# Layer 3 of a four-layer graph network: phases over neighbouring source blocks, turned pairs grouped by target, node operations on GpSimd

## The chip, the cores and the metric

The kernel is one launch on one core of a Trainium2 chip. The time is the device time of the launch in microseconds; for the kernel before it is 658.86 us, the median of 3 runs (657.34 to 660.25). Each engine of the core (TensorE for matrix products, VectorE, ScalarE and GpSimd for elementwise work, SyncE for transfers) runs its own instructions in the order in which the program issues them, and waits for the others through semaphores. The profile calls them PE (PEld for its weight loads), DVE, ACT, POOL and SP.

## The reference

The input is 3327 nodes of 64 features and a dense 3327 x 3327 matrix `adj`, mostly zero. Four layers follow one another: a gated graph network of two rounds, a hyperbolic one, one with rank weights, and a hyperbolic one with attention, which is the one changed. Each is added to `x`:

```python
h = jnp.maximum(_layernorm(x, axis=-1), 0.0)
x = x + _L3_gnn_ref(h, adj, L3_gnn_att_W, L3_gnn_att_b)

def _L3_gnn_ref(x, adj, att_W, att_b):
    x_tan = _logmap0(x, C)
    left = x_tan @ att_W[:D] + att_b
    right = x_tan @ att_W[D:]
    adj_att = jax.nn.sigmoid(left + right.T) * adj
    x_local = _logmap(x[:, None, :], x[None, :, :], C)
    support_t = jnp.einsum('ij,ijd->id', adj_att, x_local)
    return _proj(_expmap(x, support_t, C), C)
```

`_logmap(p1, p2)` of two nodes is a combination of both, with a factor that depends on their norms and distance. So every pair (i, j) needs a distance and an attention; but the distance is the same for (i, j) and (j, i).

## The kernel before

The nodes are padded to 26 blocks of 128. A column block `c` (0 to 12) is two of them, b = 0 and 1. Group `gs_` holds column blocks 0 to 5, group `gf` 6 to 12. Layers 0 to 2 stream `adj` from memory through the products; layer 3 reads `adj3`, a copy that the host lays out in the order of use.

Layer 3 works through 91 pairs of column blocks in 13 **phases** of 7 pairs (`Phase`, L131 on): four within `gf`, six between the groups (source one block of `gs_`, all seven of `gf` as targets), three within `gs_`. A phase has two halves b. A half takes these steps, each a function marked `step3`:

- `distances`: TensorE, in chunks of 4 and 3 pairs, into a pair of PSUM banks; `gelus` (ScalarE) brings them out through a Gelu, `square` (ScalarE) squares what is left: a fit of the factor of the logarithm. The result tile is s0 to s3.
- `tanh_d` (L1355), `attention_d` (L1392), `factors_d` (L1410): the attention of the direct pairs by a tanh on ScalarE, times `adj` and then times the factor on VectorE; `gather_d` and `singles` are the products that sum over sources (L1438, with the features `xd` and with `p2c`).
- the **turned** pairs, the same distance for the other direction: `turned` (L1422) transposes the squares 64 by 64 on TensorE into the other pair of banks; `tanh_t` (L1379) makes the attention, one instruction for each pair; `attention_t`, `factors_t` (L1429, reading PSUM) and `gather_t` follow, four pairs at a time (a chunk u). A pair of a block with itself has no turned one.

Before that the nodes need their own values. `nodes3` is a generator that runs once for each group and is advanced by the letters `n` (gf) and `s` (gs_): layer norm, norms, the transposed features `xs` and their swapped copy `xw` (four transfers issued by GpSimd), packed rows for the distances (`par`, `ab`, `pack`, then transposes to `rows_i` and `rows_j`), and `leftb`. For `gs_` it begins where layer 2 ends, while the phases within `gf` run. `b` is the bound that picks the fast ending, `f` the ending of `gf`; `finish` is that of `gs_`.

The order of all steps is written out by hand in `ORDER3` and is the order of each engine's queue. In it `distances.0.1.0` is phase 0, half 1, chunk 0; `factors_t.1.0.1` is phase 1, half 0, chunk 1. PSUM has two pairs of banks (`pair(0)` for distances, `pair(1)` for transposes) and four single banks; two of these, 2 and 3, take the first two distance chunks, of phase 0 half 0, before the sums of `gf` need them.

## Time and profile before

| | |
|---|---|
| median of 3 runs | 658.86 us |
| profiled execution, its time and span | 658.55, 656.7 us |
| TensorE busy, share of the span | 611.3 us, 93% |
| VectorE | 454.3 us, 69% |
| ScalarE | 386.2 us, 59% |
| GpSimd | 9.3 us, 1% |
| mean granted TensorE clock | 0.983 |
| layer 3, first distances to the end | 410 to 656.7 us |

A row of the profile names line, engine and operation, written tile <- read tiles, shape and count, then busy microseconds and mean nanoseconds of one. A product of two float32 operands is two TensorE instructions. Numbers in brackets behind a row of the timeline are the engine's idle time before it and what ended it. TensorE's ends are modelled, so the starts are the safer reading. Other layers are not touched by the change, except that the hand-written order also covers the end of layer 2.

### The profile page before, as it was taken

The numbers are of one execution on the slowest core, as the hardware profiler recorded it, in microseconds if no ns is written. First come the engines' busy times: TensorE is split into PE (matmuls) and PEld (weight loads), VectorE is DVE, ScalarE is ACT, GpSimd is POOL, SyncE is SP. The second block draws the span as 40 slices with busy tenths as digits, with TensorE's granted clock in tenths as the row PEclk, the third lists the DMA queues.
The fourth block names the chain that finished last, engine by engine and source line by source line (L and its number), as shares of the span: only waits on it lengthen the run. The fifth ranks groups of instructions, "written<-read, shape, count | busy, mean of one in ns | idle before, by whom it ended". The sixth has DMA issues, their size and how long they took to land.

```text
span 656.7 us, 14066 instructions
## 1 busy us (share of the span) xinstructions
PE 611.3 (93%) x6004; PEld 339.1 (52%) x6004; DVE 454.3 (69%) x721; ACT 386.2 (59%) x562; POOL 9.3 (1%) x19
## 2 busy tenths in 40 slices
PE   1987999999999999889999999799999999999993
PEld 1442344344333434346667677366666666676781
DVE  3240777345488740777656865789999999999966
ACT  3110400130253501368888889889999999999914
POOL 0000000000000000010000100010000000000000
PEclk9999999999999999999999999989999999999995
DMA  8999999359996999998879897426667665666501
GB/s 337 417 365 418 372 387 343 155 201 403 418 415 276 355 412 417 418 397 316 308 246 330 279 318 255 137 82 193 210 226 249 232 252 170 226 199 194 188 2 57
DMA packets 32534, 183.46 MB, mean 279 GB/s; under 512 B 3696, under 2 KB 4752, under 8 KB 32464
## 3 DMA queue, kind: packets, MB, share of 16 engines
q1 hardware_dynamic: 32112, 181.63, 74.1%
q0 software_dynamic: 352, 0.85, 0.5%
q8 instruction: 49, 0.80, 0.5%
q14 instruction: 21, 0.17, 0.1%
HBM read 180.76 MB, written 0.85 MB: 277 GB/s over the span
## 4 chain that ended last, share of the span: by engine, by line
PE 78%; ACT 7%; DMA 6%; DVE 6%; issue 2%; SPq 0%; ACTq 0%; DVEq 0%
PE bank L730 27%; PE bank L1438 17%; PE pair L1321 7%; PE pair L1763 7%; PE bank L1785 6%; DMA adj<-in_adj 5%; PE pair L1422 4%; PE pair L831 2%; ACT w L1775 2%; PE pair L635 1%; ACT tr L1379 1%; PE bank L1535 1%; DMA xn<-in_x 1%; ACT d L1355 1%; ACT dir L1355 1%
## 5 line engine op out<-in xcount | busy, mean ns | idle before, releaser
L730 PE MATMUL bank<-adj,m_a 128*64 128x384 f32 (+1 forms) x832 | 155.0, 519 | 9.3 <-DMA adj<-in_adj 6.9
L730 PEld LDWEIGHTS bank<-adj,m_a 128*64 128x64 f32 x832 | 57.1, 138 | 96.9 <-issue 72.3
L1775 ACT ACTIVATE w<-pair,ebias 128x896 uint16<-128x896 f32 (+1 forms) x100 | 91.2, 954 | 15.2 <-PE pair L1763 14.3
L730 PE MATMUL bank<-adj,m_b 128*64 128x384 f32 (+1 forms) x416 | 76.7, 515 | 1.4 <-ACT hm L819 1.4
L458 DVE SCALAR_TENSOR_TENSOR edges<-adj,edges 128x1792 bf16<-128x1792 f32 (+1 forms) x24 | 45.0, 1890 | 30.5 <-DMA adj<-in_adj 30.4
L1732 DVE TENSOR_SCALAR mask<-adj 128x1792 bf16<-128x1792 f32 (+1 forms) x52 | 52.0, 1027 | 17.2 <-PE pair L1763 17.2
L819 ACT ACTIVATE hm<-bank 64x384 f32<-64x384 f32 (+1 forms) x8 | 4.1, 512 | 94.5 <-DVE mh L818 94.3
L1785 PE MATMUL bank<-w,m_b 128*64 128x384 bf16 (+1 forms) x416 | 56.0, 340 | 0.0
L730 PEld LDWEIGHTS bank<-adj,m_b 128*64 128x64 f32 x416 | 29.0, 137 | 45.6 <-issue 42.4
L1321 PE MATMUL pair<-xs,xw 64*128 64x512 f32 (+3 forms) x116 | 50.3, 519 | 1.6 <-ACT sq L1337 1.1
L1321 PE MATMUL pair<-xs 64*128 64x512 f32 (+3 forms) x116 | 50.3, 519 | 1.3 <-ACT sq L1337 1.1
L1392 DVE SCALAR_TENSOR_TENSOR d<-d,adj 128x1792 f32<-128x1792 f32 x19 | 38.3, 2016 | 0.0
L1785 PE MATMUL bank<-w,h_t 128*64 128x384 bf16 x208 | 37.9, 339 | 0.0
L1763 PE MATMUL pair<-mask,tri_b 128*64 128x384 bf16 (+1 forms) x208 | 37.3, 339 | 0.0
L1355 ACT ACTIVATE d<-leftb,righth 128x1792 f32<-128x1792 f32 (+6 forms) x27 | 35.2, 1337 | 0.0
L1763 PE MATMUL pair<-mask,rest_a 128*64 128x384 bf16 x192 | 33.4, 341 | 1.8 <-ACT w L1775 1.6
L1379 ACT ACTIVATE tr<-leftb,righth 128x256 f32<-128x256 f32 x82 | 34.9, 499 | 0.3 <-PE bank L1438 0.3
L1438 PE MATMUL bank<-d,xd 128*64 128x384 f32 (+3 forms) x188 | 32.2, 472 | 0.0
L1785 PEld LDWEIGHTS <-m_b 128*64 128x64 bf16 x416 | 25.9, 110 | 12.3 <-issue 1.4
L1379 ACT ACTIVATE t<-leftb,righth 128x256 f32<-128x256 f32 x74 | 31.3, 499 | 0.2 <-PE bank L1438 0.2
L1438 PE MATMUL bank<-d,p2c 128*32 128x256 f32 (+1 forms) x304 | 29.6, 345 | 0.0
L1763 PE MATMUL pair<-mask,tri_a 128*64 128x384 bf16 x208 | 27.1, 341 | 1.7 <-ACT w L1775 1.6
(336 smaller groups left out, 1100.5 us busy)
## 6 DMA issues: line engine op xcount, KB each, us to landing
adj<-in_adj SPq DMA_DIRECT2D x108, 896.0 KB, 6.2
adj<-in_adj SPq DMA_DIRECT2D x92, 768.0 KB, 8.3
adj<-in_adj SPq DMA_DIRECT2D x12, 640.0 KB, 4.1
xn<-in_x SPq DMA_DIRECT2D x3, 192.0 KB, 5.2
out<-s SPq DMA_DIRECT2D x3, 192.0 KB, 2.4
xw<-xs POOLq DMA_DIRECT2D x4, 128.0 KB, 4.8
w_l<-in_w_l SPq DMA_DIRECT2D x1, 460.0 KB, 10.0
xn<-in_x SPq DMA_DIRECT2D x1, 256.0 KB, 6.8
```

Of the source, the lines that this page charges most:

```text
L458: V.scalar_tensor_tensor(e, a, 0.0, e, op0=OP.not_equal, op1=OP.add)
L730: T.matmul(acc[q][h * D : (h + 1) * D, : hi - lo], lhsT=m[:, k, :], rhs=a[:, h * g.w + lo : h * g.w + hi], start=first, stop=last,)
L1321: T.matmul(p[k][:, o : o + n], lhsT=l, rhs=r, start=not rows, stop=rows)
L1355: S.activation(columns(dirs[m, b], ph.n)[:, :, first * P : first * P + n], left_of(ph.g)[:, :, o : o + n], AF.Tanh, bias=righth[:, 2 * c + ...
L1379: S.activation(a[:, 8 * u * P : (8 * u + 2 * n) * P].rearrange("p (r x c) -> p x r c", r=2, c=D)[:, 2 * i : 2 * i + 2], left_of(ph.s)[:, : ...
L1392: V.scalar_tensor_tensor(a[:, :w], a[:, :w], 1.0, stream.tile(stream.now), op0=OP.add, op1=OP.mult)
L1422: T.transpose(p[:, r * 512 + o : r * 512 + o + D], a[rs], ident[rs, rs])
L1438: T.matmul(out, lhsT=lhsT, rhs=rhs, start=False, stop=True, skip_group_check=True)
L1732: V.tensor_scalar(masks[n][:, :w], a, 0.0, None, op0=OP.not_equal)
L1763: T.matmul(cnt[h][s * D : (s + 1) * D, P + lo : P + hi], lhsT=l, rhs=r, start=first and j == 0, stop=j == len(terms) - 1 or first and s == ...
L1775: S.activation(w, e, AF.Relu, bias=ebias)
L1785: T.matmul(acc2[i][q][h * D : (h + 1) * D, : hi - lo], lhsT=p[:, 2 * c + a, :], rhs=ws[n][:, h * g.w + lo : h * g.w + hi].bitcast(BF16), s ...
```

## The change

`Phase` takes several (source, targets) runs. Between the groups a phase now has two neighbouring sources, with four and three targets, in place of one source with seven; within the groups the 91 pairs are likewise cut anew. Turned pairs of one target block whose sources are neighbours form a group: one tanh, and products over both, where there was one for each. Chunks hold whole groups, up to four pairs. The first distance chunks lie in other banks: (phase 0, half 0, chunk 0) and (0, 1, 1) in the single banks, (0, 0, 1) in `pair(1)`. Phase 0's square is done on VectorE as a * (a + 2 HG), and the constant HG^2 is added with the next factor. In `nodes3` of `gs_`, `E` is GpSimd: the small operations on SBUF go there; copies from PSUM and the relu go to ScalarE. `singles` mixes direct and turned products by the columns done so far. The host's layout of `adj3` follows, and `ORDER3` is written anew.

```diff
@@ -132,28 +132,54 @@
 
 
 
-    def __init__(self, cs, targets):
-        self.runs = []
-        self.cols, self.turned = [], []
-        for c in cs:
-
-            ts = [o for o in targets if c not in targets or o >= c]
+    def __init__(self, *sources):
+        self.runs, self.cols = [], []
+        by_j = {}
+        for c, ts in sources:
+            ts = list(ts)
             self.runs.append((c, ts, len(self.cols)))
             for o in ts:
                 if o != c:
-                    self.turned.append((len(self.cols), c, o))
+                    by_j.setdefault(o, []).append((c, len(self.cols)))
                 self.cols.append((c, o))
-        self.g = next(g for g in GROUPS if targets[0] in g.cs)
-        self.s = next(g for g in GROUPS if cs[0] in g.cs)
-        self.n, self.nt = len(self.cols), len(self.turned)
-
-
-COLS = [list(g.cs) for g in GROUPS]
-PHASES = [Phase(cs, COLS[1]) for cs in ((9, 10), (8, 11), (7, 12), (6,))]
+
+        groups = []
+        for j, entries in by_j.items():
+            for c, i in sorted(entries):
+                if groups and groups[-1][0] == j and groups[-1][1] + groups[-1][2] == c:
+                    groups[-1][2] += 1
+                    groups[-1][3].append(i)
+                else:
+                    groups.append([j, c, 1, [i]])
+        groups.sort(key=lambda g: -g[2])
+        self.turned, x = [[]], 0
+        for j, c, n, i in groups:
+            if sum(g[2] for g in self.turned[-1]) + n > 4:
+                self.turned.append([])
+            self.turned[-1].append((j, c, n, i, x))
+            x += 2 * n
+        self.g = next(g for g in GROUPS if self.runs[0][1][0] in g.cs)
+        self.s = next(g for g in GROUPS if self.runs[0][0] in g.cs)
+        self.n, self.nt = len(self.cols), x // 2
+
+
+r_ = range
+PHASES = [
+    Phase((6, r_(6, 10)), (7, r_(7, 10))),
+    Phase((9, r_(9, 11)), (11, r_(11, 13)), (8, r_(8, 11))),
+    Phase((6, r_(10, 13)), (12, r_(12, 13)), (7, r_(10, 13))),
+    Phase((8, r_(11, 13)), (9, r_(11, 13)), (10, r_(10, 13))),
+]
 BETWEEN = len(PHASES)
-PHASES += [Phase((c,), COLS[1]) for c in COLS[0]]
+for _c in range(0, 6, 2):
+    PHASES.append(Phase((_c, r_(6, 10)), (_c + 1, r_(6, 9))))
+    PHASES.append(Phase((_c + 1, r_(9, 13)), (_c, r_(10, 13))))
 WITHIN = len(PHASES)
-PHASES += [Phase(cs, COLS[0]) for cs in ((0, 5), (1, 4), (2, 3))]
+PHASES += [
+    Phase((0, r_(0, 4)), (1, r_(1, 4))),
+    Phase((0, r_(4, 6)), (1, r_(4, 6)), (4, r_(4, 6)), (5, r_(5, 6))),
+    Phase((2, r_(2, 6)), (3, r_(3, 6))),
+]
 
 
...
+SINGLE3 = ((0, 0, 0), (0, 1, 1))
+BY_V3 = (0,)
...
-    weigh.51.0 weigh.49.1 weigh.50.1 weigh.51.1 wk distances.0.1.0 distances.0.1.1
-    attention_t.0.0 attention_d.0.0 tanh_t.0.1.1 attention_t.0.1 square.0.0 evict s clear.0
-    clear.2 gelus.0.1.0 clear.1 tanh_t.1.0.0 factors_d.0.0 distances.1.0.0 s s s gelus.0.1.1
-    square.0.1 turned.0.0.0 gelus.1.0.0 s distances.1.0.1 factors_t.0.0.0 turned.0.0.1 s s
...
+    count.51.0 count.51.1.1 weigh.49.1 distances.0.0.0 attention_t.0.0 gelus.0.0.0
+    distances.0.0.1 weigh.50.0 weigh.51.0 gelus.0.0.1 attention_d.0.0 square.0.0 weigh.50.1
+    weigh.51.1 wk evict distances.0.1.0 s s s tanh_t.1.0.0 gelus.0.1.0 tanh_d.0.1
+    distances.1.0.0 gelus.1.0.0 distances.0.1.1 s clear.2 distances.1.0.1 gelus.0.1.1 s
+    clear.1 factors_d.0.0 clear.0 square.0.1 gelus.1.0.1 gather_d.0.0 s s turned.0.0.0
+    factors_t.0.0.0 distances.1.1.0 gather_t.0.0.0 turned.0.0.1 attention_t.0.1
+    factors_t.0.0.1 gather_t.0.0.1 singles.0.0 s s tanh_d.1.0 turned.0.1.0 gelus.1.1.0
+    factors_t.0.1.0 distances.1.1.1 s turned.0.1.1 attention_d.0.1 factors_d.0.1 square.1.0
+    factors_t.0.1.1 gelus.1.1.1 distances.2.0.0 s s tanh_t.1.1.0 gather_t.0.1.0 s
+    attention_t.1.0 attention_d.1.0 s s gelus.2.0.0 distances.2.0.1 s s square.1.1
+    gather_t.0.1.1 turned.1.0.0 factors_t.1.0.0 tanh_d.1.1 attention_t.1.1 s s gather_d.0.1
+    gelus.2.0.1 distances.2.1.0 factors_d.1.0 tanh_d.2.0 singles.0.1 gather_t.1.0.0
+    gelus.2.1.0 turned.1.1.0 factors_t.1.1.0 square.2.0 distances.2.1.1 tanh_t.2.0.0
+    gelus.2.1.1 s tanh_t.2.0.1 s gather_d.1.0 square.2.1 distances.3.0.0 s gelus.3.0.0
...
@@ -713,7 +740,7 @@
-                if q:
+                if q or g is gs_:
                     S.activation(m[:, a:b], acc[q][:, : b - a], AF.Identity, bias=bias)
@@ -1071,6 +1098,7 @@
+        E = G if g is gs_ else V
...
@@ -1082,8 +1110,10 @@
         V.scalar_tensor_tensor(xc, bc(mean), -1.0 / D, x, op0=OP.mult, op1=OP.add)
         yield
         S.activation(sq, xc, AF.Square)
-        V.tensor_scalar(hr, xc, 0.0, None, op0=OP.max)
-        if g is gf:
+        if g is gs_:
+            S.activation(hr, xc, AF.Relu)
+        else:
+            V.tensor_scalar(hr, xc, 0.0, None, op0=OP.max)
 
             V.tensor_scalar(hr[:, g.nb - 1, :], hr[:, g.nb - 1, :], lastf, None, op0=OP.max)
...
             dst = par[:, i, :].rearrange("p (a c) -> p a c", a=2)
-            V.tensor_scalar(dst, by_halves(a), mul, add, op0=OP.mult, op1=OP.add)
+            E.tensor_scalar(dst, by_halves(a), mul, add, op0=OP.mult, op1=OP.add)
 
         put(0, qv, 1.0, 0.0)
...
-            V.tensor_copy(xs[:, cs], p[:, :n])
+            if g is gs_:
+                S.activation(xs[:, cs], p[:, :n], AF.Copy)
+            else:
+                V.tensor_copy(xs[:, cs], p[:, :n])
...
-            V.tensor_copy(ab[:, i], par)
+            E.tensor_copy(ab[:, i], par)
             if i < 2:
-                V.tensor_sub(par, par, ab[:, i])
+                E.tensor_sub(par, par, ab[:, i])
         yield
...
-        V.tensor_copy(pi[:, :, 0:3, :], twice(ab[:, 0, 0, :], 3))
...
+        E.tensor_copy(pi[:, :, 0:3, :], twice(ab[:, 0, 0, :], 3))
...
-                if i:
+                if i or g is gs_:
...
+        E.tensor_scalar(p2c[:, sl, ROWS - 1], qv, 2.0, 2.0, op0=OP.mult, op1=OP.add)
...
-            if i % 2:
+            if i % 2 or g is gs_:
...
-        if (m, b) == (0, 0):
+        if (m, b, i) in SINGLE3:
             p = pts[m, b, i] = [bank(2), bank(3)]
         else:
-            q = pts[m, b, i] = pair(0)
+            q = pts[m, b, i] = pair(int((m, b, i) == (0, 0, 1)))
             p = [q[:, :512], q[:, 512:]]
...
         a = columns(sqs[m, b], PHASES[m].n)[:, :, lo * P : hi * P]
-        if (m, b) == (0, 0):
+        if (m, b, i) in SINGLE3:
...
         a = sqs[m, b][:, : 2 * PHASES[m].n * P]
-        S.activation(a, a, AF.Square, bias=hg)
+        if m in BY_V3:
+            V.scalar_tensor_tensor(a, a, 2.0 * HG, a, op0=OP.add, op1=OP.mult)
+        else:
+            S.activation(a, a, AF.Square, bias=hg)
+
+    def rest_of(m):
+
+        return HD + HG * HG if m in BY_V3 else HD
 
     def left_of(g):
...
-    def some(m, u):
-
-        return list(enumerate(PHASES[m].turned))[4 * u : 4 * u + 4]
+    def of_chunk(m, u):
+
+        groups = PHASES[m].turned[u]
+        return groups[0][4], 2 * sum(g[2] for g in groups)
+
+    def by_rows(a, m, u):
+
+        x, n = of_chunk(m, u)
+        return a[:, x * P : (x + n) * P].rearrange("p (r x c) -> p x r c", r=2, c=D)
 
     @step3
     def tanh_t(m, k, u):
@@ -1373,14 +1419,11 @@
             trs[m, k] = wide3("tr", f"t{count3[0] % 4}")
             count3[0] += 1
         a = trs[m, k]
-        n = len(some(m, u))
-        for i, (_, (_, c, j)) in enumerate(some(m, u)):
-            o = (c - ph.s.c0) * P
+        for j, c, n, _, x in ph.turned[u]:
+            o, x = (c - ph.s.c0) * P, x - ph.turned[u][0][4]
             S.activation(
-                a[:, 8 * u * P : (8 * u + 2 * n) * P].rearrange("p (r x c) -> p x r c", r=2, c=D)[
-                    :, 2 * i : 2 * i + 2
-                ],
-                left_of(ph.s)[:, :, o : o + P].rearrange("p b (r c) -> p b r c", r=2),
+                by_rows(a, m, u)[:, x : x + 2 * n].rearrange("p (b e) r c -> p b e r c", b=2),
+                left_of(ph.s)[:, :, o : o + n * P].rearrange("p b (e r c) -> p b e r c", r=2, c=D),
                 AF.Tanh,
                 bias=righth[:, 2 * j + k : 2 * j + k + 1],
...
             cs = slice(lo * P, hi * P)
-            V.scalar_tensor_tensor(a[:, :, cs], s[:, :, cs], HD, a[:, :, cs], op0=OP.add, op1=OP.mult)
+            V.scalar_tensor_tensor(
+                a[:, :, cs], s[:, :, cs], rest_of(m), a[:, :, cs], op0=OP.add, op1=OP.mult
+            )
 
     @step3
     def turned(m, k, u):
 
         p = pts[m, k, "t"] = pair(1)
-        for e, (i, _, _) in some(m, u):
-            for b in range(2):
-                o = (2 * (e - 4 * u) + b) * D
-                a = columns(sqs[m, b], PHASES[m].n)[:, k, i * P : (i + 1) * P]
-                for r in range(2):
-                    rs = slice(r * D, (r + 1) * D)
-                    T.transpose(p[:, r * 512 + o : r * 512 + o + D], a[rs], ident[rs, rs])
+        groups = PHASES[m].turned[u]
+        for _, _, n, cols, x in groups:
+            for e, i in enumerate(cols):
+                for b in range(2):
+                    o = (x - groups[0][4] + b * n + e) * D
+                    a = columns(sqs[m, b], PHASES[m].n)[:, k, i * P : (i + 1) * P]
+                    for r in range(2):
+                        rs = slice(r * D, (r + 1) * D)
+                        T.transpose(p[:, r * 512 + o : r * 512 + o + D], a[rs], ident[rs, rs])
 
     @step3
     def factors_t(m, k, u):
-        n = len(some(m, u)) * 2 * D
-        p = pts.pop((m, k, "t")).rearrange("p (r c) -> p r c", r=2)[:, :, :n]
-        a = trs[m, k][:, 8 * u * P : 8 * u * P + 2 * n].rearrange("p (r c) -> p r c", r=2)
-        V.scalar_tensor_tensor(a, p, HD, a, op0=OP.add, op1=OP.mult)
-
-    def factors_of(m, k, e, b):
-
-        u, n = e // 4, len(some(m, e // 4)) * 2
-        a = trs[m, k][:, 8 * u * P : (8 * u + n) * P].rearrange("p (r x c) -> p x r c", r=2, c=D)
-        return a[:, 2 * (e % 4) + b]
+        x, n = of_chunk(m, u)
+        p = pts.pop((m, k, "t")).rearrange("p (r c) -> p r c", r=2)[:, :, : n * D]
+        a = trs[m, k][:, x * P : (x + n) * P].rearrange("p (r c) -> p r c", r=2)
+        V.scalar_tensor_tensor(a, p, rest_of(m), a, op0=OP.add, op1=OP.mult)
 
     def add(out, lhsT, rhs):
...
     def gather_t(m, k, u):
-        for e, (_, c, j) in some(m, u):
-            p, o = place(c)
-            for b in range(2):
-                add(
-                    p[b * D : (b + 1) * D, o : o + P],
-                    xd[:, 2 * j + k, :],
-                    factors_of(m, k, e, b),
-                )
+        v = by_rows(trs[m, k], m, u)
+        for j, c, n, _, x in PHASES[m].turned[u]:
+            x -= PHASES[m].turned[u][0][4]
+            for p, o, lo, hi in runs(range(c, c + n), place):
+                for b in range(2):
+                    f = x + b * n
+                    add(
+                        p[b * D : (b + 1) * D, o : o + (hi - lo) * P],
+                        xd[:, 2 * j + k, :],
+                        v[:, f + lo : f + hi],
+                    )
 
     def single(sums_, out, c, s, rhs):
...
                 i += n
-        for e, (_, c, j) in enumerate(PHASES[m].turned):
-            o = c % 2 * P
-            for h_ in range(2):
-                rhs = factors_of(m, b, e, h_)
-                turned_.append(((h_, b, slice(o, o + P)), c, 2 * j + b, rhs))
+        for u, (j, c, n, _, x) in ((u, g) for u, q in enumerate(PHASES[m].turned) for g in q):
+            i, v = 0, by_rows(trs[m, b], m, u)
+            x -= PHASES[m].turned[u][0][4]
+            while i < n:
+                w = min(2 - (c + i) % 2, n - i)
+                o = (c + i) % 2 * P
+                for h_ in range(2):
+                    f = x + h_ * n + i
+                    rhs = v[:, f : f + w]
+                    turned_.append(((h_, b, slice(o, o + w * P)), c + i, 2 * j + b, rhs))
+                i += w
+        done_ = [0, 0]
         while direct or turned_:
-            for q, most in ((direct, 2), (turned_, 4)):
-                for _ in range(min(most, len(q))):
-                    single(sums_, *q.pop(0))
-
+            q = (direct, turned_)
+            i = 0 if not turned_ or direct and done_[0] <= done_[1] else 1
+            for _ in range(2):
+                done_[i] += q[i][0][0][2].stop - q[i][0][0][2].start
+                single(sums_, *q[i].pop(0))
 
 
```

## The prediction

> **What bounds the kernel now.** I read the sums by stretch first. Columns: stretch, its length, busy time of TensorE, weight loads, VectorE, ScalarE and GpSimd (instructions in brackets), granted clock, DMA share, GB/s.
>
> ```profile
> 410.00:440.00 30.00, 25.20 (x247) 14.88 (x246) 24.54 (x35) 24.94 (x34) 2.06 (x4) 0.89 0.33 91
> 440.00:620.00 180.00, 178.73 (x2584) 117.53 (x2585) 172.49 (x147) 173.39 (x242) 0.00 (x0) 1.00 0.65 218
> 620.00:634.00 14.00, 14.00 (x231) 10.91 (x226) 13.06 (x11) 4.69 (x10) 0.00 (x0) 1.00 0.01 2
> 634.00:657.00 23.00, 12.63 (x90) 7.67 (x86) 11.53 (x47) 8.51 (x27) 0.00 (x0) 0.65 0.12 42
> ```
>
> Layer 3 runs from 410 to the end. From 440 to 634 three engines are nearly full: TensorE 99%, VectorE 96%, ScalarE 96% (until 620). The first 30 us are loose on all three, and the last 23 us are one dependent chain. Which of three full engines binds is settled by who waits for whom; these are TensorE's own waits of 440 to 632, all of them (line, released by, us, times, longest):
>
> ```profile
> PE pair L1321 <- ACT sq L1337: 1.1, 1, 1.1
> PE bank L1218 <- DVE leftb L1223: 0.2, 1, 0.2
> ```
>
> So TensorE waits 1.3 us in 192: it binds. ScalarE's idle time there, 6 us, ends on TensorE's distances, and its last tanh is over 9 us before TensorE's gathers. Next, the rows of the work that changes, every shape apart (mean ns of one behind the busy us), and one run of eight small tanh:
>
> ```profile
> L1379 ACT ACTIVATE tr<-leftb,righth 128x256 f32<-128x256 f32 x82 | 34.9, 499 | 0.3 <-PE bank L1438 0.3
> L1379 ACT ACTIVATE t<-leftb,righth 128x256 f32<-128x256 f32 x74 | 31.3, 499 | 0.2 <-PE bank L1438 0.2
> L1355 ACT ACTIVATE d<-leftb,righth 128x512 f32<-128x512 f32 x4 | 2.8, 708 | 0.0
> L1392 DVE SCALAR_TENSOR_TENSOR d<-d,adj 128x1792 f32<-128x1792 f32 x19 | 38.3, 2016 | 0.0
> 454.06 3.29 ACT L1379 ACTIVATE tr<-leftb,righth 128x256 f32<-128x256 f32 x8
> 504.47 2.62 PE L1438 MATMUL bank<-tr,xd 128*64 128x128 f32 x44
> 630.03 1.73 PE L1438 MATMUL bank<-dir,xd 128*64 128x256 f32 x16
> ```
>
> **Merged pairs, on TensorE: nothing.** The merge turns two 128-column products into one of 256. The last two lines price that. 44 products of 128 columns, on two halves of the array, are 2,816 columns a half in 2.62 us. The 16 of the other line (a whole direct gather, several widths) are 7 blocks x 2 passes x 128 = 1,792 columns a half in 1.73 us. Less the 0.17 us that a product outlasts its columns (273 ns at 128, 382 at 256), both are 0.87 ns a column. Weight loads are hidden, so TensorE pays for columns, and the columns stay: 78 turned and 91 direct pairs before and after, 26 half-phases. The new interleave of the node sums balances lanes that are balanced already: the trace has one half-phase at 1.67 us, 2 passes x 7 blocks x 128 columns at 0.845 plus 0.15. What falls: by the two written orders, changes between the three tile shapes of the array go from 111 to 103; each costs some 0.1 us (a 128-column step of 108 ns becomes 204 where the shape changes). That is 0.8 us.
>
> **Merged pairs, on ScalarE.** Eight small tanh take 3.29 us, so one each (3.29 - 0.50) / 7 = 0.40; 256 elements at 0.84 ns (708 - 499 over 256 more) are 0.215, the fixed part 0.185. The pairs as grouped give 88 turned tanh for 156 (24 of 256, 60 of 512, 4 of 768), the same elements: -68 x 0.185 = -12.6 us. Phases of two to four sources cut the direct tanh into 62 for 38: +24 x 0.185 = +4.4. The two squares of phase 0 leave for VectorE: -2 x 1.7 = -3.4. Taken over from VectorE for the second node chain: the relu of 768 (0.84), two copies to xs, two to rows_i, two to leftb and one eviction, 4.7 by the rows of like size. Sum -6.9 us. As TensorE waits only 1.1 us for ScalarE after 440, this buys at most that.
>
> **VectorE.** Gone: relu 0.56, eviction 0.61, xs 1.11, leftb 1.2, rows_i 1.2, and the small operations now on GpSimd (par, ab, packs, the seven behind them) 3.6 as they stand in a row: 8.3 us. Added: two squares with both inputs in SBUF, by the L1392 row 2 x 2.0 = 4.0. Net -4.3 us, all before 450. VectorE was idle 3% behind TensorE, so the total does not follow.
>
> **The start.** TensorE's holes and the clock there:
>
> ```profile
> 412.05 0.91 PE L1321 MATMUL bank<-xs 64*128 64x384 f32 x2 [0.75 <-ACT sq L1334]
> 418.56 0.59 PE L1321 MATMUL pair<-xs,xw 64*128 64x384 f32 x1 [1.11 <-ACT sq L1337]
> 426.88 0.37 PE L1422 MATMUL pair<-ident,sq 64*128 64x64 f32 x2 [2.15 <-DVE tr L1429]
> 427.00:430.00 3.00, 3.00 (x42) 2.11 (x44) 2.79 (x10) 2.86 (x4) 0.00 (x0) 0.50 0.03 5
> 433.00:436.00 3.00, 2.47 (x22) 1.23 (x18) 2.28 (x9) 1.50 (x2) 0.00 (x0) 1.00 0.00 0
> ```
>
> Holes up to 439 add to 4.8 us (0.75, 1.11, 0.26, 2.15, 0.53). Behind the 2.15 hole the clock is half from 426 to 432.8: the first node sums take 3.13 for 1.67, transposes 1.05 for 0.55, a turned gather 1.66 for 0.86, small ones 0.1: 2.9 us lost. I walk the new order through with these rows. The second chunk of distances lies in another pair and no longer waits for the first's Gelu, nor do those of (0,1): the first two holes go. The first transposes of the node chain now stand ahead of phase 1's distances, so the addition on VectorE between them is waited for: +0.7. Distances 1.0.0 wait for Gelu 0.1.0 behind a three-piece tanh: +0.85; 1.0.1 for its Gelu: +0.4. The big hole stays: the first turned factors stand in VectorE's queue behind the square 0.1, the sum of variance and the sum of h squared, and that waits for ScalarE's square, about 1.5 us (TensorE has distances 1.1.0 and the first direct gather to do meanwhile, but no more). With small ones, 3.7 of holes for 4.8 plus 2.9: 4.0 us gained if the clock holds, 1.1 if it falls again.
>
> Will it? The Trainium skill (TensorE: Matmul & The Clock Gate, part 1) halves the clock after an idle window of some 3.4 us; by that letter a 1.5 us hole is safe. The row differs: 2.15 us of hole, with short products and transposes before it, was enough. The new hole is shorter and a direct gather stands before it, so I take "holds", not surely.
>
> **GpSimd.** 25 small operations move there. No row of it beside VectorE exists; nearest is this one of 128 elements:
>
> ```profile
> 1.02 0.29 POOL masks.py:199 TENSOR_SCALAR_AFFINE_SELECT ident<-ident 128x128 f32<-128x128 f32 x1
> ```
>
> 0.3 us each. What waits: the transposes of the packs stand in TensorE's queue behind 14 of them (ab, pi, pj), and everything of TensorE behind those. Ahead of them in that queue, counted from the first ab, lie a direct gather 1.6, node sums 1.6, two chunks of distances 2.1, two groups of transposes 1.1 and turned gathers 1.1: 7.5 us of cover for 14 x 0.3 = 4.2. The rule that speaks against it is in the skill's SBUF — State Buffer (two separate sides): GpSimd and a VectorE operation with two SBUF inputs take one port pair in turns, each for its whole instruction. Attention and direct factors are such, 2.0 us each. Bounds: by the row alone no stall; by the rule at its worst each of the 14 sits out one, 14 x 2.3 - 7.5 = 25 us. VectorE has only some three such operations in that stretch, about 3.2 + 2.0 us: 4.2 + 5.2 - 7.5 = 1.9 at most in the mean case. I take 0.5, near the row, since copies from PSUM leave gaps. What VectorE loses to the lock (25 x 0.3 at most) lies in the 4.3 that it gained. The moves of xs leave the four DMA issues on GpSimd's queue (0.52 each) as they were, now among small operations; their readers are phases later.
>
> **Sum.** Against the profiled execution, 658.55 us (span 656.7 and 1.85 around it): start -4.0, tile changes -0.8, of the later waits -1.3, two turned chunks fewer (50 for 52) -0.2, GpSimd +0.5, the tail of 23 us unchanged: -5.8, 652.8. The median of the runs shown lies 0.3 higher: 653.1.
>
> **Rivals.** *The clock falls again*: gain 2.9, 656.0. For: a hole of similar kind. Against: shorter, more products before it. *TensorE closes nearly all holes*, because a lighter ScalarE delivers Gelus earlier than my walk says: 7.7 of the start, 0.8, 1.3 and 0.2 less 0 to 1: 9 to 10, 649.4. It can't be more: TensorE's columns do not shrink. For: every early wait was for ScalarE or VectorE. Against: the hole behind the chained sums. *Slower: GpSimd holds the pack transposes*. Price: each of the 14 pays a whole 2.0 us operation more often than in one case of three; the gain of 5.8 is eaten once GpSimd needs 13.8 us for them (1.0 each), and at 1.5 each (21 us) it is 13.5 - 6.3 = 7 slower, 666. *No effect on ScalarE from merging*, if one operation of 512 in the new layout cost two of 256: then +6 on ScalarE, which still ends before TensorE; time as forecast, less a us.
>
> **How the numbers follow.** Forecast 0.48 (own range 650.5 to 655.5), holes closed 0.26, clock falls again 0.16, slower 0.10. A measurement of this kernel tells about 0.5%, 3.3 us, from no change: faster is below 655.6. That is 0.46 + 0.26 + 0.03 = 0.75 faster; 0.02 + 0.13 = 0.15 same; 0.10 slower. Range 645.5 to 659: it leaves out most of the slower case and the far end of the closed holes.
>
> **What would show it.** 88 turned tanh of mostly 700 ns; ScalarE with visibly more idle time after 450 while TensorE stays at 99%; 128-column and 256-column products at one price a column; no half clock about 426; GpSimd's operations before the pack transposes near 0.3 us apart. Wrong: TensorE idle before those transposes, GpSimd steps of 2 us, or TensorE's time from 440 on shrinking by more than 3 us, which would mean that it was not columns that bound it.

## The result and the profile after

The kernel after takes 650.92 us (median of 4 runs, 650.39 to 651.57) against 658.47 us for the kernel before (4 runs in the same comparison): ratio 0.9883, 95% interval 0.9858 to 0.9909. The forecast was 653.1 us, "faster". The profiled execution takes 650.47 us with a span of 648.7, 8.0 us less than the span before; its mean granted clock is 0.988 (before 0.983).

The sums by stretch of the kernel after, the columns as before (stretch, length, busy time of TensorE, weight loads, VectorE, ScalarE and GpSimd, granted clock, DMA share, GB/s):

```profile
410.00:440.00 30.00, 27.28 (x274) 15.00 (x272) 28.75 (x35) 28.93 (x43) 4.08 (x9) 1.00 0.42 124
440.00:620.00 180.00, 179.59 (x2295) 106.44 (x2295) 172.86 (x120) 164.51 (x204) 11.90 (x21) 0.99 0.64 212
620.00:634.00 14.00, 13.53 (x146) 9.51 (x134) 6.71 (x26) 3.14 (x7) 0.00 (x0) 1.00 0.01 2
634.00:649.00 15.00, 3.36 (x4) 1.13 (x4) 7.86 (x27) 5.78 (x22) 0.00 (x0) 0.58 0.18 63
```

In the first 30 us TensorE, VectorE and ScalarE are all busier by 2.1 to 4.2 us than before, and the clock is whole (0.89 before). From 440 on TensorE is as full as it was; ScalarE has lost 9 us of work there. TensorE's waits from 430 to 626, all of them (line, released by, us, times, longest):

```profile
PE bank L1228 <- POOL pack L1213: 0.3, 1, 0.3
```

That is 0.3 us where 1.3 stood from 440 to 632 before. TensorE's holes up to 460, from its timeline (start, us, row; in brackets the idle time before it and what ended it):

```profile
415.69 0.44 PE L643 MATMUL bank<-ident,m_t 128*128 128x128 f32 x2 [0.78 <-DVE xn L1104]
418.81 0.59 PE L1354 MATMUL pair<-xs 64*128 64x384 f32 x1 [0.25 <-ACT s L1370]
...
425.35 1.08 PE L1479 MATMUL bank<-tr,xd 128*64 128x256 f32 x8 [1.06 <-DVE tr L1476]
427.22 0.44 PE L1479 MATMUL bank<-tr,xd 128*64 128x128 f32 x4 [0.52 <-DVE tr L1476]
...
445.35 0.62 PE L1228 MATMUL bank<-identb,pack 128*128 128x128 bf16 x8 [0.34 <-POOL pack L1213]
```

They add to 2.95 us, the last of them for GpSimd; without it 2.6, where the prediction walked to 3.7 plus 0.5 for GpSimd. The hole behind the turned factors is there, 1.06 instead of 1.5, and the wait for the node addition (`xn`) is 0.78, as walked; the waits for Gelus are nearly gone.

**Where the 8.0 us accrue.** Both kernels do the same TensorE columns in layer 3 (49.2 us of distances, 16.9 of turns, 73.1 of gathers and 36.6 of node sums, at 0.845 ns a column for each of the two instructions of a float32 product, half of that for a bfloat16 one, divided by the halves or quarters of the array that share the work). So I summed these columns along each trace, and read when the same amount was done:

```
point in layer 3                       before     after    after - before
first distance                         410.0      408.8     -1.1
8 us of columns done                   431.5      423.3     -8.2
20                                     450.8      442.4     -8.4
60                                     501.0      492.5     -8.5
120                                    568.7      558.7    -10.0
150                                    604.7      592.4    -12.3
165                                    624.0      612.7    -11.3
174                                    633.8      625.1     -8.7
end of the last product                636.8      628.1     -8.7
end of the span                        656.7      648.7     -8.0
```

In sum the start gives it all. Of the -7.3 between the first distance and 20 us of columns, 1.7 are only moved: the transposes of the packs come later in the order now (1.2), and one group of layer 2's products (`weigh.49.1`, 0.5) stands ahead of the first distance, where five groups stood behind it before and four do now. So the real gain of the start is 5.6. Up to 150 us of columns the lead grows by another 3.9, of which 1.9 are only moved as well: the steps `f` of the other group, 4.1 us of TensorE in all, now stand behind that point, where the order before had 1.9 of them ahead of it. There the lead falls again, by these and by a stretch at half clock (below).

### The profile page after: what moved, and what is told of

The parts are those of the page before. It is cut to its first block, busy times and chain, and to the rows that moved or that the text cites. A ratio compares the mean times of both kernels' runs of the same rounds, so it can differ in the third digit from the quotient of the medians.

```text
span 648.7 us, 13173 instructions
## 1 busy us (share of the span) xinstructions
PE 605.6 (93%) x5584; PEld 320.5 (49%) x5584; DVE 450.8 (69%) x688; ACT 378.5 (58%) x524; POOL 24.4 (4%) x44
## 4 chain that ended last, share of the span: by engine, by line
PE 75%; DVE 9%; DMA 7%; ACT 5%; issue 2%; POOL 1%; SPq 0%; DVEq 0%; ACTq 0%
PE bank L757 25%; PE bank L1479 16%; PE pair L1815 8%; PE bank L1837 7%; PE pair L1354 6%; DMA adj<-in_adj 6%; PE pair L1469 4%; PE pair L858 2%; ACT w L1827 2%; PE bank L1587 1%; PE pair L662 1%; DMA xn<-in_x 1%; DVE edges L485 1%; DVE d L1435 1%; PE bank L1228 1%
## 5 line engine op out<-in xcount | busy, mean ns | idle before, releaser
L1354 PE MATMUL pair<-xs 64*128 64x384 f32 (+3 forms) x120 | 50.2, 501 | 0.3 <-ACT s L1370 0.2
L1354 PE MATMUL pair<-xs,xw 64*128 64x384 f32 (+3 forms) x120 | 50.2, 501 | 0.1
L1395 ACT ACTIVATE d<-leftb,righth 128x768 f32<-128x768 f32 (+3 forms) x47 | 39.1, 893 | 0.2 <-PE bank L1479 0.2
L1479 PE MATMUL bank<-d,xd 128*64 128x384 f32 (+3 forms) x236 | 33.6, 426 | 0.0
L1476 DVE SCALAR_TENSOR_TENSOR tr<-pair,tr 128x1024 f32<-128x1024 f32 (+3 forms) x28 | 26.7, 954 | 5.2 <-PE pair L1469 4.8
L1479 PE MATMUL bank<-d,p2c 128*32 128x128 f32 (+1 forms) x348 | 29.9, 322 | 0.0
L1424 ACT ACTIVATE tr<-leftb,righth 128x512 f32<-128x512 f32 (+1 forms) x48 | 29.3, 660 | 0.0
```

The lines of the kernel that those rows point to most:

```text
L1354: T.matmul(p[k][:, o : o + n], lhsT=l, rhs=r, start=not rows, stop=rows)
L1395: S.activation(columns(dirs[m, b], ph.n)[:, :, first * P : first * P + n], left_of(ph.g)[:, :, o : o + n], AF.Tanh, bias=righth[:, 2 * c + ...
L1424: S.activation(by_rows(a, m, u)[:, x : x + 2 * n].rearrange("p (b e) r c -> p b e r c", b=2), left_of(ph.s)[:, :, o : o + n * P].rearrange ...
L1476: V.scalar_tensor_tensor(a, p, rest_of(m), a, op0=OP.add, op1=OP.mult)
L1479: T.matmul(out, lhsT=lhsT, rhs=rhs, start=False, stop=True, skip_group_check=True)
```

## Experiments

Theory A: the gain is made in the start, by closing TensorE's holes; from 440 on TensorE's columns set the time. Theory B: ScalarE held TensorE, so the merged tanh is the gain. B2: longer products are cheaper. C: the work moved off VectorE is the gain. In the table "against after" is the difference of the two ratios to the kernel before, times 658.5 us; as each ratio is uncertain by some 0.0025, such a difference is by about 2.5 us. The last two columns are read from the one profiled run. The first of them is the time from layer 3's first distance to the end of its last product. It leaves out what the unchanged layers did in that run: their end, the first distance, lies anywhere from 407.0 to 412.5 us. It does hold the half clock of that run, and the second gives the length of that; while TensorE is busy throughout, a stretch at half clock costs about half its length.

| run | ratio to before, interval | against after, us | layer 3's products, us | of it at half clock, us |
|---|---|---|---|---|
| before | | | 226.8 | 6.8 |
| after | 0.9883 [0.9858, 0.9909] | | 219.3 | 3.4 |
| one tanh a pair | 0.9922 [0.9899, 0.9946] | +2.6 | 220.5 | 0 |
| 128-column products | 0.9892 [0.9863, 0.9922] | +0.6 | 219.5 | 3.4 |
| 10.4 us more of TensorE | 1.0047 [1.0025, 1.0068] | +10.8 | 230.1 | 3.4 |
| 12 us more of VectorE | 1.0038 [1.0022, 1.0054] | +10.2 | 227.8 | 0 |
| small node operations on VectorE | 0.9924 [0.9901, 0.9946] | +2.7 | 220.2 | 0 |
| all moves undone | 1.0101 [1.0075, 1.0128] | +14.4 | 231.5 | 13.7 |
| old banks | 0.9924 [0.9899, 0.9949] | +2.7 | 222.8 | 6.8 |
| square on ScalarE | 0.9913 [0.9879, 0.9948] | +2.0 | 221.3 | 3.4 |
| xs copies on VectorE | 1.0001 [0.9977, 1.0024] | +7.8 | 227.4 | 13.7 |
| phases and order alone | 1.0151 [1.0117, 1.0185] | +17.6 | 236.8 | 13.7 |
| `f` spread | 0.9907 [0.9872, 0.9942] | +1.6 | 221.5 | 3.4 |
| before, hole filled | 0.9998 [0.9981, 1.0016] | | 225.1 | 0 |

### What binds: one tanh a pair, single products, more work on each engine

One tanh a pair (kernel after, `tanh_t`):

```diff
-            S.activation(
-                by_rows(a, m, u)[:, x : x + 2 * n]...,
-                left_of(ph.s)[:, :, o : o + n * P]...,
-                AF.Tanh, bias=..., scale=0.5)
-            yield
+            for e in range(n):
+                S.activation(
+                    by_rows(a, m, u)[:, x : x + 2 * n]...[:, :, e],
+                    left_of(ph.s)[:, :, o + e * P : o + (e + 1) * P]...,
+                    AF.Tanh, bias=..., scale=0.5)
+                yield
```

> The changed kernel, with one tanh for each turned pair again (156 for 88); products, order and all else as changed. ScalarE gets 68 x 0.185 = 12.6 us back. Theory A (the gain is made in the start, and from 440 on TensorE's columns bind): 0 to 2 us slower than the changed kernel, 651 to 653, because ScalarE has 15 idle us between 440 and 620. Theory B (ScalarE held TensorE, and merging the tanh made the gain): 6 to 9 us slower, 657 to 660.

Measured 653.31 us (652.8 to 654.38), between A's end and B's beginning, nearer to A. The rows of ScalarE for two pairs at once in after, then with one tanh a pair:

```profile
L1424 ACT ACTIVATE tr<-leftb,righth 128x512 f32<-128x512 f32 x36 | 24.1, 713 | 0.0
L1424 ACT ACTIVATE t<-leftb,righth 128x512 f32<-128x512 f32 x24 | 16.1, 712 | 0.0
```

```profile
L1425 ACT ACTIVATE tr<-leftb,righth 128x256 f32<-128x256 f32 x84 | 36.3, 519 | 0.0
L1425 ACT ACTIVATE t<-leftb,righth 128x256 f32<-128x256 f32 x72 | 30.7, 518 | 0.0
```

And TensorE's waits of 445 to 626 with one tanh a pair:

```profile
PE pair L1354 <- ACT sq L1370: 1.0, 3, 0.4
PE pair L1354 <- ACT s L1370: 0.9, 1, 0.9
PE bank L1228 <- POOL pack L1213: 0.3, 1, 0.3
```

Neighbouring operations overlap, so the busy time is read: 36.3 us for 84 is 0.43 each, 0.86 for two, where one of 512 is busy for 24.1 / 36 = 0.67. A merge saves 0.19 us, as predicted, and the rival "no effect on ScalarE" is out. Without the merge, ScalarE is busy for 175.7 of the 180 us from 440 on (after: 164.5), and TensorE waits 1.9 us for its Gelus, in after not at all. So the merge is worth about 2 to 3 us *in the new order*: 1.9 by the waits, 2.6 by the runs (no more than their uncertainty), and 2.9 by the profiles (1.2 and the 1.7 that after lost to half clock). That is more than the 1.1 that TensorE waited in the old order.

Single products (kernel after; the second edit is the same for the node sums):

```diff
-            for p, o, lo, hi in runs(range(c, c + n), place):
+            for lo in range(n):
+                hi = lo + 1
+                p, o = place(c + lo)
...
-                w = min(2 - (c + i) % 2, n - i)
+                w = 1
```

> The changed kernel, with each turned pair its own product of 128 columns again in the gathers and the node sums; the merged tanh stays. Theory A (a product costs its columns): within 1 us of the changed kernel, 651 to 652, with the gathers of 128 columns at 54 ns a step against 108 at 256. Theory B2 (fewer and longer products are worth something on TensorE): 3 us or more slower, with steps well over 54 ns.

651.78 us, +0.6: no difference that these runs can tell, with 14,197 instructions for 13,173. From 20 to 174 us of columns its profile takes 180.9 us, at full clock; after takes 182.7 there, of which half clock cost 1.7. TensorE pays for columns; B2 is out.

Ten microseconds more on TensorE, and twelve more on VectorE, in phases 4 to 9 (kernel after; both repeat work whose result is not changed by it):

```diff
+                    if not rows and i == 0 and 4 <= m <= 9:
+                        T.matmul(p[k][:, o : o + n], lhsT=l, rhs=r, start=True, stop=True)
```

> The changed kernel, with the float32 distance product of the first chunk of phases 4 to 9 made twice (the second overwrites the first): 12 chunks x 2 passes x 512 columns x 0.845 = 10.4 us more columns on TensorE, all between 450 and 590. Theory A (TensorE binds there): 9 to 11 us slower, 660 to 662. Theory B (ScalarE or VectorE binds): 0 to 5 us slower.

```diff
+        if b == 0 and 4 <= m <= 9:
+            a = dirs[m, b][:, : 2 * PHASES[m].n * P]
+            V.tensor_max(a, a, a)
```

> The changed kernel, with one more operation of 2.0 us on VectorE (the maximum of the attention with itself, which changes nothing) in half 0 of phases 4 to 9: 12 us more on VectorE between 450 and 590, where it idles about 4%, some 6 us. Theory A (TensorE binds, VectorE close behind): 5 to 8 us slower, 656 to 659. Were VectorE the bound: 12 us slower. Were it far from binding: 0 to 2.

TensorE: 662.14 us, +10.8 for 10.4 of work, so it binds one for one. VectorE: 661.28 us, +10.2 for 12, where A expected 5 to 8 and a VectorE that binds 12. A miss, a little nearer to the second. The four longest waits of TensorE from 445 to 626 with the added VectorE work:

```profile
PE pair L1472 <- DVE t L1479: 3.6, 2, 1.9
PE pair L1472 <- DVE tr L1479: 2.0, 3, 0.8
PE bank L1482 <- DVE t L1479: 1.6, 1, 1.6
PE bank L1482 <- DVE tr L1479: 1.5, 1, 1.5
```

8.7 us of waits for the turned factors. VectorE had 4.8 us of idle time from 445 to 600 in after (150.23 busy of 155), but of the 12 us added only some 2 found such room. TensorE binds, but by this run VectorE follows within about two microseconds (the uncertainty is 2.5), so a cut on TensorE alone should soon meet VectorE.

### The parts of the start: banks, square, small operations, moves

The old banks for the first distances:

```diff
-SINGLE3 = ((0, 0, 0), (0, 1, 1))
+SINGLE3 = ((0, 0, 0), (0, 0, 1))
...
-            q = pts[m, b, i] = pair(int((m, b, i) == (0, 0, 1)))
+            q = pts[m, b, i] = pair(0)
```

> The changed kernel, with the first distance chunks in the banks of before: both of phase 0 half 0 in the two single banks, those of half 1 in the pair. Theory A: the second chunk waits again for the first's Gelu (1.1 us of ScalarE) but two groups of layer 2's products follow it, and the chunk (0,1,1) waits for (1,0,0)'s Gelu: 1 to 3 us slower, 652 to 654, more if the clock falls behind the holes. If banks don't matter: within 1 us.

654.37 us, +2.7, 0.4 above what A expected (652 to 654). Its profiled run has the waits for Gelus back (1.4, 0.7 and 0.6 us) and a half clock of 6.8 us behind them, and needs 20.6 us for the first 8 us of columns, after 14.4, before 21.5.

The square of phase 0 back on ScalarE:

```diff
-BY_V3 = (0,)
+BY_V3 = ()
```

> The kernel after with the squares of phase 0 on ScalarE as before: two operations of about 1.7 us there, two of 2.0 us fewer on VectorE, all before 440 us. Theory A (the start is bound by whoever is late to TensorE, and both engines have work in a row there): TensorE waits 0 to 2 us longer for Gelus and less for VectorE: 650.5 to 653. If the square on VectorE were a cost and not a gain: 648.5 to 650.

653.82 us, 0.8 above what A expected; +2.0, which is not more than the uncertainty of the two ratios, but the profile agrees (+2.0 at as much half clock). TensorE's five longest waits of 405 to 460 there:

```profile
PE bank L1479 <- DVE tr L1476: 2.0, 2, 1.5
PE bank L643 <- DVE xn L1104: 0.8, 1, 0.8
PE bank L643 <- ACT m_t L744: 0.5, 1, 0.5
PE pair L1354 <- ACT sq L1370: 0.4, 1, 0.4
PE pair L1469 <- ACT sq L1378: 0.4, 1, 0.4
```

Three waits for ScalarE that after does not have, 1.3 us, and a longer one for VectorE behind it. In the start ScalarE holds TensorE as VectorE does: 3.4 us taken from it there bring about 2, though VectorE gets 4 us for them.

The small node operations back on VectorE:

```diff
-        E = G if g is gs_ else V
+        E = V
```

> The changed kernel, with GpSimd's 25 small node operations on VectorE again; what went to ScalarE stays there. VectorE gets some 3.6 us back between 428 and 452, GpSimd's waits of up to 2 us behind two-input operations go. Theory A: TensorE has work before it there, 0 to 2 us slower than the changed kernel, 651 to 653. Theory C (the move to GpSimd made the gain): 4 us or more slower.

653.03 us, +2.7: above the 0 to 2 that A gave it, by less than the runs can tell. Its profile has three waits of TensorE, at 444 to 466 us, that after does not have:

```profile
PE bank L1479 <- DVE d L1453: 1.1, 1, 1.1
PE pair L1469 <- DVE tr L1476: 1.1, 1, 1.1
PE pair L1469 <- ACT leftb L1254: 0.6, 1, 0.6
```

2.8 us, and the 0.3 us for GpSimd's packs is gone: the move is worth about 2.5 us, and A's reason, that TensorE has work before it there, failed. Three operations of VectorE in after, and GpSimd's timeline beside them, show what the move costs on GpSimd:

```profile
439.60 1.22 DVE L1476 SCALAR_TENSOR_TENSOR t<-pair,t 128x1024 f32<-128x1024 f32 x1
441.86 2.10 DVE L1453 SCALAR_TENSOR_TENSOR d<-s,d 128x1792 f32<-128x1792 f32 x1
445.33 2.02 DVE L1435 SCALAR_TENSOR_TENSOR d<-d,adj 128x1792 f32<-128x1792 f32 x1
```

```profile
439.96 0.22 POOL L1196 CAST ab<-par 128x48 bf16<-128x48 f32 x1
440.27 0.28 POOL L1198 TENSOR_TENSOR par<-par,ab 128x48 f32<-128x48 f32 x1
440.62 0.22 POOL L1196 CAST ab<-par 128x48 bf16<-128x48 f32 x1
440.92 1.16 POOL L1198 TENSOR_TENSOR par<-par,ab 128x48 f32<-128x48 f32 x1
442.14 1.90 POOL L1196 CAST ab<-par 128x48 bf16<-128x48 f32 x1
...
445.42 2.07 POOL L1217 COPY pack<-ab 128x24 bf16<-128x24 bf16 x1
```

The same cast takes 0.22 or 1.90 us. The two longest began inside an operation of VectorE that reads two tiles of SBUF and ended 0.1 us behind it (444.04 behind 443.96, 447.49 behind 447.35): the shared port pair, as the Trainium skill (SBUF — State Buffer (two separate sides)) has it. The short ones shown lie beside an operation that reads PSUM (`pair`). The 14 for the packs took 7.9 us, from 439.96 to 447.86, and TensorE waited 0.34 us for them; its first group of transposes needs only the first ten, its second began at 448.86.

All moves undone: the small operations, and with them the relu, the eviction and the copies to xs, rows_i and leftb back on VectorE:

```diff
-        E = G if g is gs_ else V
+        E = V
...
-            if g is gs_:
-                S.activation(xs[:, cs], p[:, :n], AF.Copy)
-            else:
-                V.tensor_copy(xs[:, cs], p[:, :n])
+            V.tensor_copy(xs[:, cs], p[:, :n])
...
-                if i or g is gs_:
+                if i:
```

> The changed kernel, with all node operations where they were, on VectorE, those on ScalarE too (relu, xs, rows_i, leftb, the eviction): 8.3 us back on VectorE, all before 462. Theory A: the sums behind which the first turned factors wait come later by the relu and the eviction, 1.2 us, and the clock may fall again: 1.5 to 5 us slower, 652 to 656. Theory C (moves are the gain): back to the time of before, 657 to 659. If moves don't matter: within 1 us.

664.39 us, 1% slower than before and far outside the three expectations. The row of TensorE's timeline that tells it:

```profile
438.54 0.66 PE L632 MATMUL bank<-ident,xd 128*128 128x128 f32 x2 [4.05 <-DVE xs L1155]
```

The second group of transposes needs the bank that the copy to `xs` empties. TensorE waits longer for VectorE elsewhere too: 2.7 us at two groups of transposes for turned factors, 1.5 for `leftb`, 1.1 for the eviction, three waits that after does not have. A new theory, D: the one copy to xs is the largest part, and what the written order leans on. It was tested by moving nothing but the copies to xs back:

```diff
-            if g is gs_:
-                S.activation(xs[:, cs], p[:, :n], AF.Copy)
-            else:
-                V.tensor_copy(xs[:, cs], p[:, :n])
+            V.tensor_copy(xs[:, cs], p[:, :n])
```

> The kernel after with only the copies of the transposed features (xs) of the second group on VectorE, as before; everything else stays. With all the moves undone TensorE waited 4.05 us for this copy, which stands behind attention and factors of 2 us each on VectorE, and the clock then fell to half. If this one wait is the larger part of the 14 us that the undone moves cost: 658 to 665. If the 14 us come from VectorE's load as a whole: 651 to 654.

659.33 us: the gain is gone. From this run, VectorE's queue ahead of the copy, then TensorE behind it, then the sums of the ten microseconds that follow:

```profile
433.51 2.02 DVE L1432 SCALAR_TENSOR_TENSOR d<-d,adj 128x1792 f32<-128x1792 f32 x1
435.57 2.02 DVE L1450 SCALAR_TENSOR_TENSOR d<-sq,d 128x1792 f32<-128x1792 f32 x1
437.51 0.42 DVE L1473 SCALAR_TENSOR_TENSOR tr<-pair,tr 128x256 f32<-128x256 f32 x1
437.84 0.68 DVE L1157 COPY xs<-bank 128x512 f32<-128x512 f32 x1
```

```profile
434.58 0.22 PE L1351 MATMUL pair<-rows_i,rows_j 64*128 64x128 bf16 x2
438.67 0.66 PE L632 MATMUL bank<-ident,xd 128*128 128x128 f32 x2 [3.86 <-DVE xs L1157]
439.26 1.98 PE L1476 MATMUL bank<-tr,xd 128*64 128x256 f32 x8
```

```profile
440.00:450.00 10.00, 10.00 (x54) 5.67 (x52) 5.83 (x8) 2.86 (x4) 6.20 (x22) 0.56 0.68 209
```

Attention and direct factors stand ahead of the copy, TensorE stands 3.86 us behind it, and then it runs at half clock for 10.24 us, which costs about 5.1. 3.9 + 5.1 = 9.0 us, where layer 3's products take 8.1 longer than in after and the runs 7.8. The half clock is no accident of this execution: all 14 have a mean clock of 0.976 to 0.983, the four of after 0.985 to 0.990. In after ScalarE starts the same copy at 431.55, 0.15 us behind its transposes. So D accounts for some 8 of the 14.4 us; the rest is with the other waits above.

Phases and order alone: all the edits of this section and of the one before together (one tanh a pair, single products, moves undone, old banks, square on ScalarE), so that only the phases, their grouping and the written order are new:

```diff
-BY_V3 = (0,)
+BY_V3 = ()
...
-        E = G if g is gs_ else V
+        E = V
```

> The kernel after with only its phases and its written order: one tanh a pair, 128-column products, the small operations on VectorE, the copies and the relu where they were, the first distances in the old banks, the square on ScalarE. Theory A (the order closes the holes of the start, and it can do so only with the work taken off VectorE, since the copies that TensorE waits for otherwise stand behind 2 us operations): as without the moves alone (664.4) plus about 2.5 for tanh and 2.7 for the banks, less what the square frees on VectorE: 663 to 670, slower than before. Rival (the order is the gain by itself, and the moves and merges are small additions to it): 653 to 657.

669.49 us, 1.5% slower than before, as A with D expected and against the rival. The written order is no gain by itself. It takes the chain of the nodes far forward between the phases, and pays only when the chain's copies don't queue behind VectorE's long operations. The other way round, the moves in the old order, was not run, so what they would bring there stays open; the prices above, which add to more than the whole gain, hold in the new order only.

### The clock

The kernel before, with the float32 products of one of its distance chunks done four times, so that TensorE has work in place of its 2.15 us hole:

```diff
+                    for _ in range(3 if not rows and (m, b, i) == (1, 0, 1) else 0):
+                        T.matmul(p[k][:, o : o + n], lhsT=l, rhs=r, start=True, stop=True)
```

> The kernel before, with the float32 product of distances 1.0.1 made four times in place of once: 2.0 us more of TensorE work, in the hole of 2.15 us at 424.7. Nothing else is changed. If that hole is what halves the clock for 6.8 us: the clock stays full and the time falls by 2 to 3 us, 655.5 to 656.5, in spite of more work. If the clock falls for another reason: 0 to 1 us slower, and half clock from 426 on as before.

```profile
410.00:440.00 30.00, 27.42 (x284) 17.07 (x282) 25.80 (x40) 26.44 (x35) 2.06 (x4) 1.00 0.39 119
```

In the profiled run the clock of the start is whole, and layer 3's products take 225.1 us, 1.7 less than before, with the same hole filled. Over all runs nothing is gained: 658.31 us, ratio 0.9998, outside both expectations. The mean granted clocks of the single runs tell more. Of the 74 runs of the kernel before in these comparisons, 39 have 0.982 to 0.986, as the profiled one (0.983), at a median of 659.6 us, and 35 have 0.987 to 0.990, at 657.8. A difference of 0.005 is what 6.8 us at half clock make of such a span, though the mean does not say where they lay. With the hole filled 13 of 14 runs have 0.988 or more; in the same comparison 14 of 21 of before have 0.987 or more, at 658.4 us. So by these means a loss of that size falls in about half of the runs, and those are some 1.8 us longer; the 2.9 us that the prediction booked for it are one execution's, and of a median about 0.9 us (an estimate: half of 1.8). That the fill keeps it away is likely, by one run in 14 against 7 in 21, and not shown.

In after the clock falls elsewhere. TensorE's timeline there has the same direct gather twice:

```profile
602.57 1.74 PE L1479 MATMUL bank<-d,xd 128*64 128x256 f32 x16
...
606.45 0.61 PE L1587 MATMUL bank<-halves,h_n 128*128 128x2 f32 x4
606.92 0.59 PE L1587 MATMUL bank<-halves,xc 128*128 128x2 f32 x4
...
609.40 3.21 PE L1479 MATMUL bank<-d,xd 128*64 128x256 f32 x16
```

3.21 us for 1.74: the granted clock is half from 609.1 to 612.5, without an idle moment of TensorE in the records before it. What stands before it are the `f` steps with products of two columns. Spreading these was tried:

```diff
-    turned.11.1.0 distances.12.1.1 gelus.12.1.1 gather_d.11.0 gather_t.11.0.0
-    gather_t.11.0.1 attention_d.11.1 factors_d.11.1 turned.11.1.1 f f factors_t.11.1.1
-    square.12.1 turned.12.0.0 gather_t.11.1.1 gather_d.11.1 tanh_d.12.0 attention_t.12.0
+    turned.11.1.0 distances.12.1.1 gelus.12.1.1 gather_d.11.0 gather_t.11.0.0 f
+    gather_t.11.0.1 f attention_d.11.1 factors_d.11.1 turned.11.1.1 factors_t.11.1.1
+    square.12.1 turned.12.0.0 gather_t.11.1.1 f gather_d.11.1 tanh_d.12.0 attention_t.12.0
...
-    factors_t.12.0.0 gather_t.12.0.0 attention_d.12.0 turned.12.0.1 factors_t.12.0.1 f f f f
+    factors_t.12.0.0 gather_t.12.0.0 attention_d.12.0 turned.12.0.1 factors_t.12.0.1 f f
...
-    attention_d.12.1 singles.11.1 singles.11.0 factors_t.12.1.0 turned.12.1.1
+    attention_d.12.1 singles.11.1 f singles.11.0 factors_t.12.1.0 turned.12.1.1
```

> The kernel after with the steps of the last node sums of the first finished group (the small products of two columns) spread one by one between gathers, instead of standing in a row of two and of four. In the profile of after TensorE runs at half clock from 608.8 to 612.2 us, without an idle moment before it, just behind these. If the crowd of small products is what brings the half clock: no half clock before the tail, 649.0 to 650.4 us, against 650.9 for after. If it is not: 650.5 to 651.7 and a half clock at about the same place.

```profile
606.00:610.00 4.00, 3.48 (x45) 2.85 (x44) 2.36 (x3) 4.00 (x4) 0.00 (x0) 1.00 0.71 229
610.00:615.00 5.00, 5.00 (x40) 3.51 (x38) 3.99 (x3) 1.43 (x3) 0.00 (x0) 0.66 0.01 3
```

653.57 us, no gain; TensorE now waits 0.52 us in there, and the clock still falls (611.2 to 614.6). That the crowd of small products is the cause has no support, though the test is weak: three rows of them still stand in the six us before. The profiled runs with one tanh a pair, with more VectorE work and with the small operations on VectorE show no half clock before the tail at all. What brings it near 609 stays open.

## Why the prediction was right, step by step

**The start, -4.0: right in kind, too small.** It is -5.6 in the profiled executions. My walk took 3.7 us of holes for the new order; 2.6 are there. The waits for Gelus, walked at 0.85 and 0.4, are down to 0.25, since the square and the shorter queue of tanh leave ScalarE freer than the walk had it, and the hole behind the chained sums is 1.06 for 1.5. The experiment with the square on ScalarE brings such waits back. Holes and clock together went from 7.7 to 2.6; the last 0.5 us of the start I can't put down to a row. The first distance comes another 1.1 earlier, which no step foresaw; it is the end of the unchanged layers, which varies by more than that from run to run.

**"The clock holds": so it did in the start**, in the profiled run. But the term of 2.9 us is one execution's: about half of the runs of before show no such loss in their mean clock. And the clock fell once, for 3.4 us, late in layer 3; that was not foreseen and costs 1.7.

**Merged products, nothing: shown**, by the single products (+0.6, inside the uncertainty).

**ScalarE's relief, "at most 1.1": the step that was wrong.** For the merge alone it is 1.9 by the waits and 2.6 by the runs. (The 0.84 ns an element in that step is 0.82 by its own two rows, 209 ns for 256, which changes nothing.) The waits of a trace bound what relief is worth in that order only. Once the start is closed, TensorE comes to each Gelu earlier, and a ScalarE with the old load would be late. That is the same error as in the next point: I priced edits against the queues of before, while the new order had spent what they freed.

**VectorE, "the total does not follow", and the moves to ScalarE, booked as 4.7 us of its work and no time.** True as a sum, but they are what the start stands on: with the copies to xs alone on VectorE the gain is lost (+7.8), with all moves undone it is worse than before. The prediction walked the new order with the moves in place and so came out right, but it gave the moves no share in the gain. Also, VectorE is nearer to binding than "3% behind" sounds: 12 us more there cost 10.2. And the bound on what VectorE loses to GpSimd was summed wrongly: 25 x 0.3 is 7.5 us, which does not lie in the 4.3 that it gained. It did no harm, for the 2.0 us operations beside GpSimd's took 2.1 us at most.

**GpSimd, +0.5: right in size, with some luck.** 0.34 us of wait, but the 14 took 7.9 us and not 4.2, nearly 0.6 each, since three of them sat out operations of VectorE; the cover held because the first transposes need only ten of them. The rival "slower, GpSimd holds the packs" needed 1.0 us on average.

**Later waits -1.3, shape changes -0.8, two chunks -0.2.** At equal columns the stretch from 20 to 174 us takes 183.0 us before and 182.7 after. Without the 1.2 of transposes moved into it and the 1.7 of half clock it would be 3.2 shorter; 2.3 was forecast. The 1.3 are seen (0.3 of waits left, and that is GpSimd's); of the rest, about 2, the changes between shapes of product that fell away (104 for 115 in that stretch) make 1.1 at the price taken, and 0.9 stays open. That was not tested by itself; fewer and longer products are not the reason, as the run with 128-column products takes no longer there.

**The tail unchanged**: 19.9 us from the last product to the end before, 20.6 after.

Between the rivals: "holes nearly all closed" (649.4) is nearer than the forecast (653.1) to the 650.92 measured, and the truth lies between the two. So the mechanism of the start was right, and the size came from terms that were too small (start 4.0 for 5.6, later stretch 2.3 for 3.2) and from two not foreseen that cancel in part (the first distance 1.1 earlier, the late half clock 1.7).

## What to carry over

Price a rewritten order and the moves that came with it as one: an operation that looks free in the old queues can be what the new order leans on, so walk each producer's queue (here a 0.7 us copy behind two 2 us operations) and not only the sums of each engine. A wait in the trace bounds what an edit gives in that order, not in the next one. To compare runs of a program whose early part is noisy, add up the bound engine's work in both traces and compare the times at equal work; the place where the lead grows is where the gain is made.

## What the runs showed of the hardware

- The clock can be halved with TensorE busy in the records: 609.1 to 612.5 us in after, in which a gather of 1.74 us took 3.21. The half-clock stretches of layer 3 that end before the tail last 3.41 us or a small multiple of it (6.83 before, 10.24 with the xs copies on VectorE, 13.65 with phases and order alone).
- The granted clock differs between executions of one program: of 74 runs of before 39 have a mean of 0.982 to 0.986 and 35 of 0.987 to 0.990, and the median of the first is 1.8 us longer.
- One and the same GpSimd operation of 48 elements took 0.22 us beside a VectorE operation that reads PSUM. Begun inside one that reads two tiles of SBUF, it took 1.90 us and ended 0.1 us behind it.
- Unchanged layers ended up to 5.5 us apart between profiled runs (first distances at 407.0 to 412.5), not much less than the 7.8 us by which the runs of before spread (656.1 to 663.9).
